# An edge layer's pair terms, laid out by quarters of the neighbours and 32 channels

## The chip, the cores and the metric

The kernel runs on one core of a Trainium2 chip. Its engines are TensorE (PE, with weight loads shown apart as PEld), VectorE (DVE), ScalarE (ACT), GpSimd (POOL) and SyncE (SP). The metric is the device time of one execution in microseconds. A measurement is the median of several runs, and one further execution was recorded by the hardware profiler; the views of the profile below are of that one.

## The reference, cut to what matters

The program is a chain of four layers on an image tensor of 4 samples, 56 rows (l), 56 columns (n) and 128 channels, in float32: an attention layer, an edge layer, a spectral layer and a convolution, each on a group-normalised input and added to it. The change touches the edge layer alone:

```python
W1, W2 = (We[:, :f], We[:, f:])                      # f = 128
proj_i = jnp.einsum('blnf,of->blno', x, W1)
proj_j = jnp.einsum('blnf,of->blno', x, W2)
edge = jax.nn.relu(proj_i[:, :, :, None, :] + proj_j[:, :, None, :, :] + be)
edge_sum = edge.sum(axis=3)
node_in = jnp.concatenate([x, edge_sum], axis=-1)
node = jax.nn.relu(jnp.einsum('blnc,oc->blno', node_in, Wn) + bn)
```

For every row l and every column n, the layer sums relu(a[n] + c[m] + be) over all 56 columns m of the same row, for each of the 128 channels. These are 4 x 56 x 56 x 56 x 128 pair terms. The sum, with x, goes through one more projection.

## The kernel before, in words

The samples are worked one after the other. For each, `fast_layer` computes the attention layer into the tile x1 and `edge_layer` works on x1 in place. Channels are the 128 partitions. The 3136 pixels of a sample are cut into 7 blocks (NBLK) of 448 (NB), 8 rows of 56, so the edge layer works 28 blocks in all.

For a block, `project` (L1184, L1186) makes two products of 448 columns in PSUM: e_pc with W2 and e_pa with W1. `evacuate` (L1194 to L1197) has ScalarE write e_c = -(e_pc) - be and e_a, a copy of e_pa, to SBUF, and prepare x for its later update. Then come 14 turns, listed in the string EDGE_TURNS. A turn makes the terms of 4 columns m at once, 128 x 1792 numbers. In the 9 "d" turns VectorE takes max(e_pa, e_c) (L1231), with e_pa read from PSUM and e_c from SBUF. As relu(a - c) = max(a, c) - c, the sum of the c of these turns is taken off later: e_rest is that sum (L1248). In the 5 "p" turns GpSimd subtracts e_c from e_a, both in SBUF (L1233), and ScalarE rectifies the result in place (L1235). All of GpSimd's operands here are in SBUF; e_a is the copy that it reads.

TensorE sums the terms by products with 32 x 32 blocks of the identity (L1238). A turn has 16 of them: one for each of its 4 columns m and each group r of 32 channels. They accumulate over all turns in the four PSUM banks of e_acc, which has a single buffer: the partitions of e_acc are the place q of m within its turn times 32 channels, its banks are the groups r. Each product is two instructions in the trace, as every float32 product here.

At the end of a block ScalarE copies e_acc to e_sums (L1250, 128 x 1792). `output` then makes e_po for the block before (L1202 to L1206): one product of x, one with e_rest and the negated weights, and four of e_sums, whose weights sum over the four places q. `project` of the block after next follows, and VectorE's `finish` (L1211) puts max(e_po, -bn) on x two blocks late, in turn 3.

The order on TensorE, ScalarE and VectorE is the order of the code (`manual_schedule`); GpSimd's is chosen when the program is built. The terms of VectorE have 7 buffers, those of GpSimd 4. e_pa and the tiles of tag "mm" (e_pc, e_po) have 2 PSUM banks each, which with e_acc makes all 8.

Of the kernel before, what the change touches and what calls it, by code (L numbers as in the profile page):

```python
# [12 lines left out]
F32 = mybir.dt.float32  # L13
AF = mybir.ActivationFunctionType
ALU = mybir.AluOpType
AX = mybir.AxisListType
# [3 lines left out]
P = 128  # L20
B = 4
HH = 56
TOK = HH * HH
NB = 448
# [8 lines left out]
def bc(ap, axis, n):  # L33

    ap = ap.unsqueeze(axis)
    shape = list(ap.shape)
    shape[axis] = n
    return ap.to_broadcast(shape)


def blk(j):
    return slice(j * NB, (j + 1) * NB)
# [149 lines left out]
def apply_norm(k, out, xt, mr):  # L192
    k.nc.vector.tensor_scalar(out, xt, mr[:, 0:1], mr[:, 1:2], ALU.subtract, ALU.mult)
# [950 lines left out]

EDGE_TURNS = "ddpddpdpddpddp"


def edge_layer(k, w, x1, st):  # L1150

    nc, tc = k.nc, k.tc
    xf = x1.rearrange("p l n -> p (l n)")
    nd = 4 * EDGE_TURNS.count("d")
    quarters = [slice(32 * q, 32 * q + 32) for q in range(4)]
    with ExitStack() as es:  # L1160
        big = es.enter_context(tc.tile_pool(name="e_big", bufs=1))
        wk = es.enter_context(tc.tile_pool(name="e_wk", bufs=2))
        psum = es.enter_context(tc.tile_pool(name="e_ps", bufs=2, space=PSUM))

        def bank():
            return psum.tile([P, 512], F32, tag="mm", name="e_mm")

        mr = group_norm_factors(k, wk, bank, st)
        xg = big.tile([P, TOK], F32, name="e_xg")
        shift = wk.tile([P, 1], F32, name="e_shift", bufs=1)  # L1170
        nc.vector.tensor_scalar(shift, mr[:, 0:1], mr[:, 1:2], -1.0, ALU.mult, ALU.mult)
        ready = {}

        def normed(j):
            if j < 2:
                apply_norm(k, xg[:, blk(j)], xf[:, blk(j)], mr)
            elif j < NBLK:
                nc.scalar.activation(xg[:, blk(j)], xf[:, blk(j)], AF.Identity, bias=shift, scale=mr[:, 1:2])

        def project(j):  # L1180
            if j >= NBLK:
                return
            pc = psum.tile([P, 512], F32, tag="mm", name="e_pc")
            nc.tensor.matmul(pc[:, :NB], w.W2, xg[:, blk(j)], start=True, stop=True)  # L1184
            pa = psum.tile([P, 512], F32, tag="pa", name="e_pa")
            nc.tensor.matmul(pa[:, :NB], w.W1, xg[:, blk(j)], start=True, stop=True)  # L1186
            ready[j] = pa, pc

        def evacuate(j):
            if j >= NBLK:  # L1190
                return
            pa, pc = ready[j]
            c = wk.tile([P, 8, HH], F32, name="e_c")
            nc.scalar.activation(c.rearrange("p l m -> p (l m)"), pc[:, :NB], AF.Identity, bias=w.nbe, scale=-1.0)  # L1194
            a = wk.tile([P, NB], F32, name="e_a")
            nc.scalar.copy(a, pa[:, :NB])  # L1196
            nc.scalar.activation(xf[:, blk(j)], xf[:, blk(j)], AF.Identity, bias=w.bn)  # L1197
            ready[j] = pa, a, c

        def output(j, rest, sums):  # L1200
            po = psum.tile([P, 512], F32, tag="mm", name="e_po")
            nc.tensor.matmul(po[:, :NB], w.Wn[:, 0, :], xg[:, blk(j)], start=True, stop=False)  # L1202
            nc.tensor.matmul(po[:, :NB].rearrange("p (l n) -> p l n", l=8), w.nWn, bc(rest, 2, HH),
                             start=False, stop=False)
            for r in range(4):
                nc.tensor.matmul(po[:, :NB], w.Wnq[:, r, :], sums[:, r, :], start=False, stop=(r == 3))  # L1206
            return po

        def finish(j, po):

            nc.vector.scalar_tensor_tensor(xf[:, blk(j)], po[:, :NB], w.nbn, xf[:, blk(j)], ALU.max, ALU.add)  # L1211

        with tc.manual_schedule(engines={mybir.EngineType.PE, mybir.EngineType.Activation, mybir.EngineType.DVE}):
            for j in range(2):
                normed(j)
            for j in range(2):
                project(j)
                evacuate(j)
            last = po = None
            for j in range(NBLK):  # L1220
                pa, a, c = ready.pop(j)
                acc = psum.tile([P, 4, 512], F32, name="e_acc", bufs=1)
                rest = wk.tile([P, 8], F32, name="e_rest")
                at = {"d": 0, "p": nd}
                for g, e in enumerate(EDGE_TURNS):
                    t = wk.tile([P, 4, 8, HH], F32, tag="e_" + e, name="e_t" + e, bufs=7 if e == "d" else 4)
                    cm = bc(c[:, :, at[e]:at[e] + 4].rearrange("p l m -> p m l"), 3, HH)
                    at[e] += 4
                    if e == "d":
                        am = bc(pa[:, :NB].rearrange("p (l n) -> p l n", l=8), 1, 4)  # L1230
                        nc.vector.tensor_tensor(t, am, cm, ALU.max)  # L1231
                    else:
                        nc.gpsimd.tensor_sub(t, bc(a.rearrange("p (l n) -> p l n", l=8), 1, 4), cm)  # L1233
                        tf = t.rearrange("p m l n -> p (m l n)")
                        nc.scalar.activation(tf, tf, AF.Relu)  # L1235
                    for q in range(4):
                        for r, o in enumerate(quarters):
                            nc.tensor.matmul(acc[quarters[q], r, :NB], k.ident[o, o],  # L1238
                                             t[o, q].rearrange("p l n -> p (l n)"),
                                             start=(g == 0), stop=(g == len(EDGE_TURNS) - 1))  # L1240
                    if g == 3 and po is not None:
                        finish(j - 2, po)
                    if g == 5 and j:
                        evacuate(j + 1)
                    if g == 8:
                        normed(j + 2)
                    if g == 9:
                        nc.vector.tensor_reduce(rest, c[:, :, 0:nd], AX.X, ALU.add)  # L1248
                sums = wk.tile([P, 4, NB], F32, name="e_sums")
                nc.scalar.copy(sums, acc[:, :, :NB])  # L1250
                if last:
                    po = output(*last)
                project(j + 2)
                last = j, rest, sums
            finish(NBLK - 2, po)
            finish(NBLK - 1, output(*last))


def edge_weights(k, w, pool):

    for n, t in (("nbe", w.be), ("nbn", w.bn), ("nWn", w.Wn[:, 1, :])):
        r = pool.tile(list(t.shape), F32, name="e_" + n)
        k.nc.vector.tensor_scalar_mul(r, t, -1.0)
        setattr(w, n, r)


def l1_host(i):
    We, Wn = i["L1_conv_We"], i["L1_conv_Wn"]
    W2 = Wn[:, P:].T.reshape(4, 1, 32, P)
    return {  # L1270
        "w1_W1": We[:, :P].T, "w1_W2": We[:, P:].T, "w1_be": i["L1_conv_be"].reshape(P, 1),
        "w1_Wn": Wn.T.reshape(2, P, P).transpose(1, 0, 2), "w1_bn": i["L1_conv_bn"].reshape(P, 1),
        "w1_Wnq": np.broadcast_to(W2, (4, 4, 32, P)).reshape(4, P, P).transpose(1, 0, 2),
    }


# [1388 lines left out]
def group_norm_factors(k, pool, bank, st):  # L2665

    nc = k.nc
    mv = pool.tile([P, 2], F32, tag="mv", name="gf_mv")
    nc.vector.bn_aggr(mv, st.rearrange("p a b -> p (a b)"))
    ps = bank()  # L2670
    nc.tensor.matmul(ps[:, 0:1], k.g4, mv[:, 0:1], start=True, stop=True)
    mr = pool.tile([P, 2], F32, tag="mr", name="gf_mr")
    nc.vector.tensor_copy(mr[:, 0:1], ps[:, 0:1])
    t = pool.tile([P, 1], F32, tag="gt", name="gf_t")
    nc.vector.tensor_sub(t, mv[:, 0:1], mr[:, 0:1])
    nc.vector.tensor_mul(t, t, t)
    nc.vector.tensor_add(t, t, mv[:, 1:2])
    ps = bank()
    nc.tensor.matmul(ps[:, 0:1], k.g4, t, start=True, stop=True)
    nc.scalar.activation(t, ps[:, 0:1], AF.Sqrt, bias=k.eps)  # L2680
    nc.vector.reciprocal(mr[:, 1:2], t)
    return mr
# [158 lines left out]
```

## Time and profile before

| | us |
|---|---|
| median of 3 runs | 3586.84 |
| lowest and highest run | 3580.55, 3589.28 |
| profiled execution, own time | 3579.81 |
| its span | 3578.0 |
| TensorE busy in the span | 3372.0 |
| VectorE busy | 2702.3 |
| ScalarE busy | 2089.9 |
| GpSimd busy | 1249.2 |
| e_td, VectorE, 252 instructions | 491.2 |
| e_tp, GpSimd, 140 instructions | 451.5 |

A group line of the profile reads: source line, engine, operation, output and inputs by the program's names, shapes, number of instructions, then busy time in us and the mean of one in ns, then the idle time of the engine just ahead of them and what ended it. A line of a timeline reads: start in us from the span's beginning, length in us, and the instructions merged in it. "Releaser" is what ended an engine's wait. Shares of busy time are means over stages with different limits, so the prediction reads the edge layer's own stretches.

### The profile page before, as it was taken

How to read it: one execution, taken by the hardware profiler on the slowest of the kernel's cores; microseconds unless marked ns; L12 is line 12 of the kernel's file. 1: busy time of each engine (PE TensorE's matmuls, PEld its weight loads, DVE VectorE, ACT ScalarE, POOL GpSimd, SP SyncE). 2: the span in 40 equal slices, each digit the busy share in tenths (PEclk: the TensorE clock that was granted, in tenths of full speed). 3: DMA queues.
4: the chain of work that ended last, by engine and by line, in shares of the span. 5: the costliest groups of instructions: out<-in, count | busy, mean ns of one | idle time of the engine just before them, and what ended most of it. 6: DMA issues, size and time to landing. Idle time of an engine off the chain costs nothing.

```text
span 3578.0 us, 80873 instructions
## 1 busy us (share of the span) xinstructions
PE 3372.0 (94%) x36096; PEld 1549.4 (43%) x36096; DVE 2702.3 (76%) x2531; ACT 2089.9 (58%) x2103; POOL 1249.2 (35%) x752
## 2 busy tenths in 40 slices
PE   6999998989999898999999999999898899999998
PEld 4433344553333455333344643333456443336664
DVE  6588868767888696688859758887784678886776
ACT  4688865458888564688856458887552112214442
POOL 1000017600000581000018400000673778884686
PEclk8999999999999999999999999999998999999999
DMA  2144420014333000444310024442103027763101
GB/s 103 43 92 92 95 42 20 20 47 94 88 88 83 20 3 20 99 93 94 89 44 3 20 57 94 94 94 63 38 3 101 15 53 178 181 148 91 55 19 55
DMA packets 98076, 244.51 MB, mean 68 GB/s; under 512 B 64456, under 2 KB 69832, under 8 KB 92712
## 3 DMA queue, kind: packets, MB, share of 16 engines
q0 software_dynamic: 16128, 102.77, 14.2%
q1 hardware_dynamic: 74872, 123.64, 11.9%
q10 hardware_dynamic: 6720, 12.85, 1.3%
q8 instruction: 285, 4.67, 0.5%
q14 instruction: 71, 0.58, 0.1%
HBM read 79.46 MB, written 31.33 MB: 31 GB/s over the span
## 4 chain that ended last, share of the span: by engine, by line
PE 79%; DVE 10%; ACT 4%; issue 4%; POOL 3%; DMA 0%; POOLq 0%; DVEq 0%; ACTq 0%
PE f_pm L818 17%; PE f_pm L684 15%; PE u_po L1878 8%; PE e_acc L1238 7%; PE q_acc L1732 3%; DVE e_td L1231 3%; PE f_pm L791 2%; PE e_po L1206 2%; PE f_pm L770 2%; ACT f_ring L821 1%; PE f_pm L464 1%; PE o_d L2141 1%; DVE f_acc L673 1%; PE o_d L2538 1%; PE f_pm L715 1%
## 5 line engine op out<-in xcount | busy, mean ns | idle before, releaser
L821 ACT ACTIVATE f_ring<-f_pm 128x1792 f32<-128x1792 f32 (+1 forms) x764 | 1093.8, 1482 | 228.7 <-PE f_pm L818 181.2
L673 DVE TENSOR_TENSOR f_acc<-f_acc,f_ring 128x1792 f32<-128x1792 f32 x468 | 947.7, 2025 | 191.1 <-ACT f_ring L821 160.9
L818 PE MATMUL f_pm<-f_qT,f_kT 32*128 32x448 f32 x5376 | 725.2, 571 | 15.5 <-ACT f_ring L821 5.1
L684 PE MATMUL f_pm<-f_ring,f_va 128*32 128x448 f32 (+1 forms) x6304 | 589.4, 490 | 0.0
L663 POOL DMA_DIRECT2D f_far<-f_ring x112 | 96.6, 862 | 1329.3 <-ACT f_ring L821 1108.2
L1231 DVE TENSOR_TENSOR e_td<-e_pa,e_c 128x1792 f32<-128x1792 f32 x252 | 491.2, 2018 | 14.1 <-ACT e_a L1196 14.1
L1233 POOL TENSOR_TENSOR e_tp<-e_a,e_c 128x1792 f32<-128x1792 f32 x140 | 451.5, 3261 | 101.4 <-PE e_acc L1238 59.8
L818 PEld LDWEIGHTS f_pm<-f_qT,f_kT 32*128 32x128 f32 x5376 | 260.4, 183 | 417.2 <-ACT f_ring L821 304.7
L1238 PE MATMUL e_acc<-e_td,t_shared 32*32 32x448 f32 x8064 | 325.8, 545 | 24.9 <-DVE e_td L1231 24.0
L684 PEld LDWEIGHTS f_pm<-f_ring,f_va 128*32 128x32 f32 x6304 | 164.2, 109 | 409.7 <-issue 397.4
L1873 DVE TENSOR_TENSOR u_ud<-u_px,u_d 112x1792 f32<-112x1792 f32 x144 | 263.5, 1864 | 39.6 <-PE u_po L1878 35.4
L1235 ACT ACTIVATE e_tp<-e_tp 128x1792 f32<-128x1792 f32 x140 | 233.4, 1694 | 74.0 <-POOL e_tp L1233 74.0
L1875 POOL TENSOR_TENSOR u_up<-xh,u_d 112x1792 f32<-112x1792 f32 (+1 forms) x72 | 240.9, 3376 | 55.0 <-PE u_po L1878 39.7
L1238 PE MATMUL e_acc<-e_tp,t_shared 32*32 32x448 f32 x4480 | 222.6, 544 | 3.0 <-ACT e_tp L1235 2.4
L1878 PE MATMUL u_po<-u_ud,AT 112*64 112x448 f32 x1056 | 213.8, 544 | 1.9 <-DVE u_ud L1873 1.9
L1238 PEld LDWEIGHTS e_acc<-e_td,t_shared 32*32 32x32 f32 x8064 | 142.3, 103 | 138.4 <-DVE e_td L1231 79.4
L1878 PEld LDWEIGHTS u_po<-u_ud,AT 112*64 112x64 f32 x1056 | 74.4, 138 | 128.8 <-issue 112.9
L1250 ACT COPY e_sums<-e_acc 128x1792 f32<-128x1792 f32 x28 | 46.3, 1652 | 136.2 <-PE e_acc L1238 136.2
L1238 PEld LDWEIGHTS e_acc<-e_tp,t_shared 32*32 32x32 f32 x4480 | 96.5, 103 | 53.0 <-issue 16.6
L728 DVE RECIPROCAL f_den<-f_den 128x448 f32<-128x448 f32 x28 | 82.6, 2951 | 44.1 <-ACT f_den L725 44.1
L1717 POOL TENSOR_TENSOR q_u<-iS,q_g 128x1792 f32<-128x1792 f32 x32 | 102.8, 3236 | 23.0 <-PE q_acc L1732 22.8
L1732 PE MATMUL q_acc<-q_u,S 64*64 64x448 f32 x1024 | 104.6, 553 | 4.4 <-DVE q_u L1719 3.3
(525 smaller groups left out, 4511.6 us busy)
## 6 DMA issues: line engine op xcount, KB each, us to landing
f_far<-f_ring POOLq DMA_DIRECT2D x112, 896.0 KB, 6.3
u_d<-dd SPq DMA_DIRECT2D x46, 784.0 KB
f_far<-f_ring SPq DMA_DIRECT2D x28, 896.0 KB
xw<-in_x SPq DMA_DIRECT2D x4, 1568.0 KB
x2d<-x SPq DMA_DIRECT2D x4, 1568.0 KB
xat<-x SPq DMA_DIRECT2D x4, 1568.0 KB
x_xs<-xat ACTq DMA_DIRECT2D x32, 196.0 KB
xm<-x_ev ACTq DMA_DIRECT2D x64, 98.0 KB
```

The lines of the kernel that those rows point to most:

```text
L673: nc.vector.tensor_add(e.acc, e.acc, slots(j, c))
L684: nc.tensor.matmul(e.po[heads[h], part], va[o, c, heads[h]], p, start=(c == 0), stop=(c == 23 and part.stop == NB))
L818: nc.tensor.matmul(ss[:, i, :NB], kT[heads[h], c * P:(c + 1) * P], qT[heads[h], blk(j)], start=True, stop=True)
L821: nc.scalar.activation(ring[:, slot:slot + m, :], ss[:, :m, :NB], AF.Exp, scale=scale)
L1231: nc.vector.tensor_tensor(t, am, cm, ALU.max)
L1233: nc.gpsimd.tensor_sub(t, bc(a.rearrange("p (l n) -> p l n", l=8), 1, 4), cm)
L1235: nc.scalar.activation(tf, tf, AF.Relu)
L1238: nc.tensor.matmul(acc[quarters[q], r, :NB], k.ident[o, o], t[o, q].rearrange("p l n -> p (l n)"), start=(g == 0), stop=(g == len(EDGE_TUR ...
L1732: nc.tensor.matmul(acc[bp][i][halves[hb % 2], hb // 2, :NB], x[o], u[o, 8 * hb:8 * hb + 8, :].rearrange("p h t -> p (h t)"), start=first, ...
L1873: nc.vector.tensor_mul(u, bc(px[:, :, :NB], 2, m), dm)
L1875: nc.gpsimd.tensor_mul(u, bc(x, 2, m), dm)
L1878: nc.tensor.matmul(po[64 * b2:64 * b2 + 64, :NB], st.AT[:, 8 * i + h0 + q, 2 * bp + b2, :], u[:, b2, q, :], start=(left == 16), stop=(left ...
```

## The change

The terms are laid out in another way. The 56 columns m are cut into 4 quarters of M = 14. The partitions of a term are now (quarter q of m, 32 channels) and its free axes are (channel group r, row l, column n). A turn g takes the columns m = g, 14 + g, 28 + g and 42 + g together.

- `project` makes e_pc in 16 products of 112 columns (32 channels by 14 columns m of 8 rows each), and e_pa in four products of 448, each with weights that hold 32 channels of W1 four times over. e_pa takes four banks, with one buffer.
- `evacuate` has ScalarE write e_c = -(e_pc) and the four groups of e_a = e_pa + be to SBUF. Of these, the second two come later, in turn 8.
- VectorE's and GpSimd's terms both read e_a and e_c, which are in SBUF.
- Of the 14 turns, 8 are VectorE's, 5 GpSimd's, and one, "s", is shared: VectorE makes its groups r = 0 and 1, GpSimd its groups 2 and 3, 128 x 896 numbers each.
- TensorE sums a term with four products of 128 rows by 32 columns: S is the 32 x 32 identity four times over, so a product sums the four quarters and leaves the group's 32 channels. e_acc is one bank with two buffers. The c terms of VectorE's turns (e_rest, now two reductions) are taken off in e_acc by four products with -S.
- e_sums is 128 x 448, and `output` has two products instead of six.
- In the first block of a layer, VectorE's first two turns are made group by group, so that they can begin with the first group of e_a.
- `edge_weights` no longer negates be and the second half of Wn; the buffers of VectorE's terms are 6 and 2 (half terms), those of GpSimd's 4 and 2.

The diff, cut to its core:

```diff
-EDGE_TURNS = "ddpddpdpddpddp"
+EDGE_TURNS = "ddpddpsdpdpddp"
...
         def project(j):
...
             pc = psum.tile([P, 512], F32, tag="mm", name="e_pc")
-            nc.tensor.matmul(pc[:, :NB], w.W2, xg[:, blk(j)], start=True, stop=True)
-            pa = psum.tile([P, 512], F32, tag="pa", name="e_pa")
-            nc.tensor.matmul(pa[:, :NB], w.W1, xg[:, blk(j)], start=True, stop=True)
-            ready[j] = pa, pc
-
-        def evacuate(j):
+            xm = xg[:, blk(j)].rearrange("p (l m) -> p l m", l=8)
+            for r, o in enumerate(quarters):
+                for q in range(4):
+                    nc.tensor.matmul(pc[quarters[q], 8 * M * r:8 * M * (r + 1)].rearrange("p (l m) -> p l m", l=8),
+                                     w.W2[:, o], xm[:, :, M * q:M * (q + 1)], start=True, stop=True)
+            pa = psum.tile([P, 4, 512], F32, name="e_pa", bufs=1)
+            for r in range(4):
+                nc.tensor.matmul(pa[:, r, :NB], w.W1[:, r, :], xg[:, blk(j)], start=True, stop=True)
+            c = wk.tile([P, 4, 8, M], F32, name="e_c")
+            a = wk.tile([P, 4, NB], F32, name="e_a")
+            ready[j] = pc, pa, c, a
+
+        def evacuate(j, part):
...
-            c = wk.tile([P, 8, HH], F32, name="e_c")
-            nc.scalar.activation(c.rearrange("p l m -> p (l m)"), pc[:, :NB], AF.Identity, bias=w.nbe, scale=-1.0)
-            a = wk.tile([P, NB], F32, name="e_a")
-            nc.scalar.copy(a, pa[:, :NB])
-            nc.scalar.activation(xf[:, blk(j)], xf[:, blk(j)], AF.Identity, bias=w.bn)
-            ready[j] = pa, a, c
+            pc, pa, c, a = ready[j]
+            if part == 0:
+                nc.scalar.activation(c.rearrange("p r l m -> p (r l m)"), pc[:, :NB], AF.Identity, scale=-1.0)
+            for r in range(2 * part, 2 * part + 2):
+                nc.scalar.activation(a[:, r, :], pa[:, r, :NB], AF.Identity, bias=w.be[:, r:r + 1])
+            if part == 1:
+                nc.scalar.activation(xf[:, blk(j)], xf[:, blk(j)], AF.Identity, bias=w.bn)
+
+        def terms(j, m, t, r0, r1, e):
...
+            _, _, c, a = ready[j]
+            cm = bc(c[:, r0:r1, :, m], 3, HH)
+            am = a[:, r0:r1, :].rearrange("p r (l n) -> p r l n", l=8)
+            if e == "d":
+                nc.vector.tensor_tensor(t, am, cm, ALU.max)
+            else:
+                nc.gpsimd.tensor_sub(t, am, cm)
+                tf = t.rearrange("p r l n -> p (r l n)")
+                nc.scalar.activation(tf, tf, AF.Relu)
...
             nc.tensor.matmul(po[:, :NB], w.Wn[:, 0, :], xg[:, blk(j)], start=True, stop=False)
-            nc.tensor.matmul(po[:, :NB].rearrange("p (l n) -> p l n", l=8), w.nWn, bc(rest, 2, HH),
-                             start=False, stop=False)
-            for r in range(4):
-                nc.tensor.matmul(po[:, :NB], w.Wnq[:, r, :], sums[:, r, :], start=False, stop=(r == 3))
+            nc.tensor.matmul(po[:, :NB], w.Wn[:, 1, :], sums, start=False, stop=True)
...
             for j in range(NBLK):
-                pa, a, c = ready.pop(j)
-                acc = psum.tile([P, 4, 512], F32, name="e_acc", bufs=1)
-                rest = wk.tile([P, 8], F32, name="e_rest")
+                acc = psum.tile([P, 512], F32, name="e_acc")
+                rest = wk.tile([P, 4, 8], F32, name="e_rest")
...
-                    cm = bc(c[:, :, at[e]:at[e] + 4].rearrange("p l m -> p m l"), 3, HH)
-                    at[e] += 4
-                    if e == "d":
-                        am = bc(pa[:, :NB].rearrange("p (l n) -> p l n", l=8), 1, 4)
-                        nc.vector.tensor_tensor(t, am, cm, ALU.max)
+                    if g in early:
+                        parts = [(early[g], 0)]
+                    elif e == "s":
+                        parts = [(tile_of("d", 2), 0), (tile_of("p", 2), 2)]
+                        for t, r in parts:
+                            terms(j, m, t, r, r + 2, "p" if r else "d")
                     else:
-                        nc.gpsimd.tensor_sub(t, bc(a.rearrange("p (l n) -> p l n", l=8), 1, 4), cm)
-                        tf = t.rearrange("p m l n -> p (m l n)")
-                        nc.scalar.activation(tf, tf, AF.Relu)
-                    for q in range(4):
-                        for r, o in enumerate(quarters):
-                            nc.tensor.matmul(acc[quarters[q], r, :NB], k.ident[o, o],
-                                             t[o, q].rearrange("p l n -> p (l n)"),
-                                             start=(g == 0), stop=(g == len(EDGE_TURNS) - 1))
+                        parts = [(tile_of(e), 0)]
+                        terms(j, m, parts[0][0], 0, 4, e)
+                    for t, r0 in parts:
+                        for r in range(t.shape[1]):
+                            nc.tensor.matmul(acc[quarters[r0 + r], :NB], w.S[:, 0, :], t[:, r].rearrange("p l n -> p (l n)"),
+                                             start=(g == 0), stop=False)
...
-                sums = wk.tile([P, 4, NB], F32, name="e_sums")
-                nc.scalar.copy(sums, acc[:, :, :NB])
+                for r in range(4):
+                    nc.tensor.matmul(acc[quarters[r], :NB].rearrange("p (l n) -> p l n", l=8), w.S[:, 1, :],
+                                     bc(rest[:, r, :], 2, HH), start=False, stop=True)
+                sums = wk.tile([P, NB], F32, name="e_sums")
+                nc.scalar.copy(sums, acc[:, :NB])
```

More of the change, by code (lines that the diff above doesn't have):

```diff
@@ L1157, in edge_layer @@
     xf = x1.rearrange("p l n -> p (l n)")
-    nd = 4 * EDGE_TURNS.count("d")
+    M = HH // 4
+    nd, ns = EDGE_TURNS.count("d"), EDGE_TURNS.count("s")
     quarters = [slice(32 * q, 32 * q + 32) for q in range(4)]
@@ L1190, in evacuate @@
+            pa = psum.tile([P, 4, 512], F32, name="e_pa", bufs=1)
[5 more added lines that the diff above has]
+        def evacuate(j, part):
             if j >= NBLK:
                 return
-            pa, pc = ready[j]
-            c = wk.tile([P, 8, HH], F32, name="e_c")
@@ L1194, in evacuate @@
-            nc.scalar.activation(c.rearrange("p l m -> p (l m)"), pc[:, :NB], AF.Identity, bias=w.nbe, scale=-1.0)
-            a = wk.tile([P, NB], F32, name="e_a")
-            nc.scalar.copy(a, pa[:, :NB])
-            nc.scalar.activation(xf[:, blk(j)], xf[:, blk(j)], AF.Identity, bias=w.bn)
-            ready[j] = pa, a, c
-        def output(j, rest, sums):
+            pc, pa, c, a = ready[j]
+            if part == 0:
+                nc.scalar.activation(c.rearrange("p r l m -> p (r l m)"), pc[:, :NB], AF.Identity, scale=-1.0)
@@ L1201, in output, with tile_of @@
+        def tile_of(e, n=4):
+            return wk.tile([P, n, 8, HH], F32, tag="e_%s%d" % (e, n), name="e_t" + e,
+                           bufs=2 if n < 4 else 6 if e == "d" else 4)
+        def output(j, sums):
             po = psum.tile([P, 512], F32, tag="mm", name="e_po")
             nc.tensor.matmul(po[:, :NB], w.Wn[:, 0, :], xg[:, blk(j)], start=True, stop=False)
-            nc.tensor.matmul(po[:, :NB].rearrange("p (l n) -> p l n", l=8), w.nWn, bc(rest, 2, HH),
-                             start=False, stop=False)
@@ L1215, in edge_layer @@
                 normed(j)
-            for j in range(2):
-                project(j)
-                evacuate(j)
+            project(0)
+            for part in range(2):
+                evacuate(0, part)
+            project(1)
             last = po = None
             for j in range(NBLK):
-                pa, a, c = ready.pop(j)
-                acc = psum.tile([P, 4, 512], F32, name="e_acc", bufs=1)
-                rest = wk.tile([P, 8], F32, name="e_rest")
-                at = {"d": 0, "p": nd}
-                for g, e in enumerate(EDGE_TURNS):
-                    t = wk.tile([P, 4, 8, HH], F32, tag="e_" + e, name="e_t" + e, bufs=7 if e == "d" else 4)
-                    cm = bc(c[:, :, at[e]:at[e] + 4].rearrange("p l m -> p m l"), 3, HH)
-                    at[e] += 4
-                    if e == "d":
-                        am = bc(pa[:, :NB].rearrange("p (l n) -> p l n", l=8), 1, 4)
-                        nc.vector.tensor_tensor(t, am, cm, ALU.max)
-                    else:
-                        nc.gpsimd.tensor_sub(t, bc(a.rearrange("p (l n) -> p l n", l=8), 1, 4), cm)
-                        tf = t.rearrange("p m l n -> p (m l n)")
-                        nc.scalar.activation(tf, tf, AF.Relu)
-                    for q in range(4):
-                        for r, o in enumerate(quarters):
-                            nc.tensor.matmul(acc[quarters[q], r, :NB], k.ident[o, o],
-                                             t[o, q].rearrange("p l n -> p (l n)"),
-                                             start=(g == 0), stop=(g == len(EDGE_TURNS) - 1))
@@ new lines, in edge_layer @@
+                acc = psum.tile([P, 512], F32, name="e_acc")
+                rest = wk.tile([P, 4, 8], F32, name="e_rest")
+                at = {"d": 0, "p": nd + ns, "s": nd}
+                early = {g: tile_of("d") for g in range(2)} if j == 0 else {}
+                for r in range(4 if early else 0):
+                    for g, t in early.items():
+                        terms(j, at["d"] + g, t[:, r:r + 1], r, r + 1, "d")
+                for g, e in enumerate(EDGE_TURNS):
+                    m = at[e]
+                    at[e] += 1
+                    if g in early:
[4 more added lines that the diff above has]
+                            terms(j, m, t, r, r + 2, "p" if r else "d")
+                    else:
+                        parts = [(tile_of(e), 0)]
[4 more added lines that the diff above has]
+                                             start=(g == 0), stop=False)
@@ L1241, in edge_layer @@
                     if g == 3 and po is not None:
                         finish(j - 2, po)
-                    if g == 5 and j:
-                        evacuate(j + 1)
+                    if g == 5:
+                        evacuate(j + 1, 0)
                     if g == 8:
+                        evacuate(j + 1, 1)
+                    if g == 10:
                         normed(j + 2)
-                    if g == 9:
-                        nc.vector.tensor_reduce(rest, c[:, :, 0:nd], AX.X, ALU.add)
@@ L1249, in edge_layer @@
-                sums = wk.tile([P, 4, NB], F32, name="e_sums")
-                nc.scalar.copy(sums, acc[:, :, :NB])
+                    if g == 8:
+                        if ns:
+                            nc.vector.tensor_reduce(rest[:, 0:2], ready[j][2][:, 0:2, :, 0:nd + 1], AX.X, ALU.add)
+                        nc.vector.tensor_reduce(rest[:, 2 if ns else 0:4], ready[j][2][:, 2 if ns else 0:4, :, 0:nd], AX.X, ALU.add)
+                for r in range(4):
+                    nc.tensor.matmul(acc[quarters[r], :NB].rearrange("p (l n) -> p l n", l=8), w.S[:, 1, :],
+                                     bc(rest[:, r, :], 2, HH), start=False, stop=True)
@@ L1253, in edge_layer @@
                 project(j + 2)
-                last = j, rest, sums
+                last = j, sums
             finish(NBLK - 2, po)
@@ L1259, in edge_weights @@
 def edge_weights(k, w, pool):
[L1261 to L1264, printed above, removed]
+    w.nbn = pool.tile([P, 1], F32, name="e_nbn")
+    k.nc.vector.tensor_scalar_mul(w.nbn, w.bn, -1.0)
 def l1_host(i):
     We, Wn = i["L1_conv_We"], i["L1_conv_Wn"]
-    W2 = Wn[:, P:].T.reshape(4, 1, 32, P)
+    W1 = np.broadcast_to(We[:, :P].T.reshape(P, 4, 1, 32), (P, 4, 4, 32)).reshape(P, 4, P)
+    S = np.tile(np.eye(32, dtype=np.float32), (4, 1))
     return {
-        "w1_W1": We[:, :P].T, "w1_W2": We[:, P:].T, "w1_be": i["L1_conv_be"].reshape(P, 1),
+        "w1_W1": W1, "w1_W2": We[:, P:].T, "w1_be": np.tile(i["L1_conv_be"].reshape(4, 32).T, (4, 1)),
         "w1_Wn": Wn.T.reshape(2, P, P).transpose(1, 0, 2), "w1_bn": i["L1_conv_bn"].reshape(P, 1),
-        "w1_Wnq": np.broadcast_to(W2, (4, 4, 32, P)).reshape(4, P, P).transpose(1, 0, 2),
+        "w1_S": np.stack((S, -S), 1),
     }
```

## The prediction

> **What bounds the kernel now.** I read the page first: the chain that ended last and the costliest groups.
>
> ```profile
> PE 79%; DVE 10%; ACT 4%; issue 4%; POOL 3%; DMA 0%; POOLq 0%; DVEq 0%; ACTq 0%
> ...
> L1231 DVE TENSOR_TENSOR e_td<-e_pa,e_c 128x1792 f32<-128x1792 f32 x252 | 491.2, 2018 | 14.1 <-ACT e_a L1196 14.1
> L1233 POOL TENSOR_TENSOR e_tp<-e_a,e_c 128x1792 f32<-128x1792 f32 x140 | 451.5, 3261 | 101.4 <-PE e_acc L1238 59.8
> ...
> L1250 ACT COPY e_sums<-e_acc 128x1792 f32<-128x1792 f32 x28 | 46.3, 1652 | 136.2 <-PE e_acc L1238 136.2
> ```
>
> TensorE carries four fifths of the chain. The edge layer runs four times (once per sample) over seven blocks, 28 blocks in all. So I asked for the busy time of each engine in two blocks of the first one (columns: stretch, its length, then PE, PEld, DVE, ACT, POOL).
>
> ```profile
> 599.74:619.42 19.68, 19.68 (x481) 11.72 (x474) 18.42 (x12) 12.08 (x11) 16.14 (x5) 1.00 0.01 3
> 619.42:639.10 19.68, 19.68 (x481) 11.71 (x474) 18.42 (x12) 12.09 (x11) 16.14 (x5) 1.00 0.01 3
> ```
>
> A block takes 19.68 us and TensorE is busy in all of it: 14 turns of about 0.96 (13.5), twelve e_po instructions start to start 0.376 (4.5), four for e_pc and e_pa (1.5). VectorE has 18.42, GpSimd 16.14, almost all of it side by side. That overlap is what matters here. VectorE's max reads e_pa, which is in PSUM, and e_c in SBUF; GpSimd's subtraction reads e_a and e_c, both in SBUF. Beside it GpSimd stretches nothing: the 252 instructions of e_td lie between 2.014 and 2.027 us.
>
> **What the trace says of two SBUF inputs.** The change makes VectorE read e_a instead of e_pa, so I looked for places where VectorE reads two SBUF tensors while GpSimd does too. They are few and agree. Timelines of VectorE, then GpSimd (start us, us):
>
> ```profile
> 2857.87 1.09 DVE L1758 TENSOR_TENSOR y<-y,q_red 128x896 f32<-128x896 f32 x1
> ...
> 2860.28 2.68 DVE L1766 TENSOR_TENSOR y<-y,q_den 128x896 f32<-128x896 f32 x1
> ```
>
> ```profile
> 2857.92 4.09 POOL L1717 TENSOR_TENSOR q_u<-iS,q_g 128x1792 f32<-128x1792 f32 x1
> 2869.70 3.19 POOL L1717 TENSOR_TENSOR q_u<-iS,q_g 128x1792 f32<-128x1792 f32 x1 [7.69 <-PE q_acc L1732]
> ```
>
> L1717 began 0.05 us behind L1758 and took 4.09 instead of 3.19: it lost the 0.9 us that a product of 1.09 needs. Then L1766, started while L1717 ran, took 2.68 instead of 1.09: it ended 0.95 us after L1717 did, and 896 elements need about that. So the two run one after the other, whichever began first, and nothing is gained from the overlap but the waiting one's fixed 0.14 us. The end of each sample's MLP shows it again:
>
> ```profile
> 542.06 1.02 DVE L799 SCALAR_TENSOR_TENSOR xf<-xf,t_first,xw 128x392 f32<-128x392 f32 x1
> ```
>
> ```profile
> 541.75 0.91 POOL L804 TENSOR_TENSOR x<-xf,xw 128x343 f32<-128x343 f32 x1 [3.95 <-DVE xf L793]
> 542.62 0.58 POOL L805 TENSOR_TENSOR x<-xf,xw 128x28 f32<-128x28 f32 x1
> ```
>
> L799 (0.63 for its like, L793, with a PSUM input) waits for L804 to end at 542.66; L805 (0.24 in its other executions) then waits for L799 to end at 543.08. All four samples show the same. And where GpSimd has work queued back to back, VectorE gets no turn between: this subtraction of one element per partition needs 0.16 us and sat through nine GpSimd instructions.
>
> ```profile
> 2723.54 5.46 DVE L1458 TENSOR_TENSOR s_t<-s_mv,s_mr 128x1 f32<-128x1 f32 x1
> ```
>
> The Trainium skill (page "SBUF — State Buffer", section "Who interferes with whom") speaks against this change in the same sense: VectorE's second SBUF read and GpSimd share a port, and whoever has it keeps it for the whole instruction. It goes further than these few rows, as it says so of every such pair; by the rule a block costs the sum of both engines' times, worked out below from rows as 34.2 us, and without it the longer one, 17.9.
>
> **The change part by part**, for one block.
>
> *VectorE and GpSimd.* Nine and five turns become 8.5 and 5.5. Back to back, VectorE's spacing is 1.93 us (five took 9.74, the last 2.02 of it), GpSimd's 3.22 (five in 16.14, the last 3.26). For half a turn the nearest rows are VectorE's 128x896 (1.09, about 1.00 back to back) and GpSimd's 128x896, L1758 (1.69, about 1.65). Held port time: VectorE 8 x 1.93 + 1.00 = 16.4; GpSimd 5 x 3.22 + 1.65 = 17.75. Sum **34.2**. Lower end: with strict alternation each hides its fixed part (1.88 and 0.95, 3.05 and 1.50): 32.7. Upper end: VectorE's one-input work, finish 0.68 and two small reduces at up to 0.3, is not covered by a GpSimd term: 35.5. I take 34.2, the back-to-back rows, since GpSimd was seen to keep its turn while it has work; the one-input instructions then lie beside GpSimd.
>
> *TensorE.* A turn becomes four products of 128 rows by 32 columns (eight instructions for 32). That form is in the trace: L684 starts a group of four heads, eight instructions, 0.70 us after the one before. 14 turns and the four products with e_rest: 15 x 0.70 = 10.5. e_po: four instructions instead of twelve, 1.5. e_pa: eight instead of two, 3.0. e_pc: sixteen pieces of 112 columns on four column groups, about 0.7. Sum 15.7, 4 us less than now, but hidden: the pair of engines needs 34.2.
>
> *ScalarE.* 5.5 rectifications (9.3), e_c 0.63, four e_a at 0.53, x 0.67, e_xg 0.75, e_sums of 448 elements about 0.53: 14. Hidden as well.
>
> *Waits and buffers.* e_acc is now doubled, so TensorE no longer waits for e_sums; that costs and brings nothing under 34.2. Behind a VectorE term that waits for GpSimd stand finish and the reduces, for which nobody hurries. With six and four buffers, one of the two engines has work whenever the other is short of a buffer, so I count the port as never idle.
>
> *Ends of a layer.* Start: TensorE runs four e_pa products at a low clock (granted 0.61 between 549.2 and 553.6) and VectorE starts in pieces of 448: +0.8. End: before, VectorE's last term ended at 687.5 and the layer at 699.7, 12.2 us, with e_sums 1.65 and two e_po groups of 4.5. After: last turn and e_rest 1.9, the older e_po 1.5, the last 1.5, finish 0.68: 5.7 with e_sums beside it.
>
> *Sum.* The first layer began its terms at 553.7. After: 553.7 + 0.8 + 7 x 34.2 + 5.7 = 799.6 against 699.7, +99.9; four layers **+400**. The profiled execution took 3579.81 us, its span 3578.0; the median of the runs is 3586.84, 7 more. A change of 400 gives 3980 there and **3987** against the median.
>
> The edits at the start of the kernel (one VectorE negation of 128x128 less, a pack of other size) are below a microsecond and I count them as nothing; no DMA is moved.
>
> **Rivals.**
>
> *The exclusion doesn't hold for this pair* (it is shown here by a handful of instructions, none of them a stream). Then a block is bound by the longer of VectorE (16.4 + 0.68 + 0.6 = 17.7) and GpSimd (17.75), with handovers 17.9. A layer: 553.7 + 0.8 + 7 x 17.9 + 5.7 = 685.5, 14.2 less; four give -57: **3530**. It decides as soon as e_td stays at 2.02 beside e_tp. For it: TensorE, which is the bound now, is relieved by 4 us a block. Against it: every pair in the trace with two SBUF inputs on both sides. This is the case on the other side.
>
> *The exclusion holds and the port also idles.* If GpSimd's runs leave TensorE and ScalarE to catch up while both producers lack buffers, one rectification and one turn, 1.7 + 0.75, are added once or twice a block: 28 x 2.45 to 4.9 = 69 to 137 more, **4056 to 4124**. For it: L1458, one engine kept out for long. Against it: ten buffered turns.
>
> *TensorE's clock drops because it idles.* At the 0.61 of the layer's start, 15.7 becomes 25.7, still under 34.2; only the ends of a layer grow, by about 3 us each, 12 in all. That is inside the range.
>
> That the change would not do what it says is out: e_td's first operand is the SBUF tile e_a in the diff.
>
> **How the numbers follow.** Forecast 0.80: 32.7 to 35.5 a block, with 3 us more at each layer's end for the upper one, give 3944 to 4035. Idle port 0.12, no exclusion 0.06, something between that cancels 0.02. The range goes a little below the first and takes in half of the second: 3925 to 4085. A difference of 0.3% is about what a measurement of this kernel can tell from none: faster 0.06, same 0.02, slower 0.92.
>
> **What the profile after would show.** Right: e_td and e_tp both longer in the mean than 2.02 and 3.26, with the excess of one lying under the other; blocks of about 34 us with TensorE busy in about half; the attention layers and all behind the edge layer unchanged. Wrong: e_td at 2.02 with blocks near 18 (first rival), or blocks over 36 with gaps on both VectorE and GpSimd (second). The TensorE step is wrong if a turn takes much more than 0.7 us of starts; it would not show in the time.

## The result, and the profile after

| | before | after |
|---|---|---|
| median of 4 runs, us | 3585.96 | 3981.27 |
| lowest and highest | 3580.55, 3589.28 | 3977.35, 3995.76 |
| profiled execution, its span | 3579.81, 3578.0 | 3984.77, 3983.0 |
| the four edge layers together | 603.5 | 1002.4 |
| all the rest of the span | 2974.5 | 2980.6 |

The changed kernel takes 1.1116 times as long, with a 95% interval of 1.1093 to 1.1139. The forecast was 3987. The last two rows are read off the timelines: an edge layer runs from the start of e_shift (VectorE, L1171 before, L1173 after) to the end of its last update of x (L1211 before, L1234 after). The edge layers take 398.9 us more; the rest differs by 6, and in the runs below, which change the edge layer alone, it lies between 2965 and 2987, so those 6 are no finding.

The page of the kernel after: the chain that ended last by engine, then the groups that answer to those shown of before.

```profile
PE 63%; DVE 23%; issue 7%; ACT 4%; POOL 2%; DMA 0%; DVEq 0%; POOLq 0%; ACTq 0%
...
L1216 DVE TENSOR_TENSOR e_td<-e_a,e_c 128x1792 f32<-128x1792 f32 (+2 forms) x276 | 924.6, 3412 | 28.1 <-ACT e_a L1206 28.1
L1218 POOL TENSOR_TENSOR e_tp<-e_a,e_c 128x1792 f32<-128x1792 f32 (+1 forms) x168 | 716.2, 4287 | 239.3 <-PE e_acc L1266 176.7
...
L1284 ACT COPY e_sums<-e_acc 128x448 f32<-128x448 f32 x28 | 14.9, 532 | 525.1 <-PE e_acc L1281 525.1
```

VectorE's share of the chain went from 10% to 23%. The mean of e_td rose from 2018 to 3412 ns although it now contains half and quarter terms, the mean of e_tp from 3261 to 4287 ns. Busy time here contains waiting inside the instruction, so a longer instruction is not more work. GpSimd was idle for 239 us ahead of its terms, 177 of them until TensorE had used up an older one and its buffer was free (the rest was the wait for e_a at the four starts), so it was not the only limit; VectorE was hardly ever idle, with 28 us ahead of its terms in four layers.

The busy time of each engine in the first edge layer and in two stretches of about a block (stretch, length, then PE, PEld, DVE, ACT, POOL, granted clock):

```profile
556.70:799.40 242.70, 151.58 (x1086) 44.89 (x1076) 237.62 (x91) 90.47 (x94) 179.26 (x46) 0.81 0.00 1
585.00:619.00 34.00, 21.57 (x168) 6.66 (x160) 34.00 (x10) 13.27 (x14) 31.78 (x8) 0.75 0.00 0
650.00:687.00 37.00, 23.34 (x176) 6.84 (x168) 37.00 (x10) 17.97 (x19) 35.11 (x9) 0.83 0.00 1
```

VectorE is busy all the time in both stretches of blocks, TensorE in under two thirds, where it was busy throughout a block before. The terms of the seven blocks run from 556.70 to 792.96, 33.75 us a block against 19.68. The last column but two, the granted clock, is below full speed. It doesn't make the loss: TensorE is free for a third of these stretches and VectorE doesn't wait for it. More on the clock at the end.

How the two engines take turns is seen in a timeline of some 20 us, VectorE first, then GpSimd. The second line of each is one instruction alone. The first of VectorE's five is shorter (3.54 us): beside it GpSimd made only a half term.

```profile
654.17 23.52 DVE L1216 TENSOR_TENSOR e_td<-e_a,e_c 128x1792 f32<-128x1792 f32 x5
...
657.63 5.07 DVE L1216 TENSOR_TENSOR e_td<-e_a,e_c 128x1792 f32<-128x1792 f32 x1
```

```profile
655.79 20.03 POOL L1218 TENSOR_TENSOR e_tp<-e_a,e_c 128x1792 f32<-128x1792 f32 x4
...
660.78 5.03 POOL L1218 TENSOR_TENSOR e_tp<-e_a,e_c 128x1792 f32<-128x1792 f32 x1
```

From there on GpSimd starts one every 5.0 us and VectorE too: the term at 657.63 ends at 662.70, that of GpSimd at 660.78 began 1.9 us before this and ends 3.1 us after it. Each instruction is 5.05 us long, of which it works 1.9 (VectorE) or 3.1 (GpSimd) and waits the rest.

### The profile page after: what moved, and what is told of

It is laid out like the page before. It is cut to its first block, busy times and chain, and to the rows that moved or that the text cites. A ratio compares the mean times of both kernels' runs of the same rounds, so it can differ in the third digit from the quotient of the medians.

```text
span 3983.0 us, 64261 instructions
## 1 busy us (share of the span) xinstructions
PE 3443.8 (86%) x27696; PEld 1439.5 (36%) x27696; DVE 3140.5 (79%) x2581; ACT 2123.2 (53%) x2215; POOL 1514.5 (38%) x780
## 4 chain that ended last, share of the span: by engine, by line
PE 63%; DVE 23%; issue 7%; ACT 4%; POOL 2%; DMA 0%; DVEq 0%; POOLq 0%; ACTq 0%
DVE e_td L1216 16%; PE f_pm L818 16%; PE f_pm L684 14%; PE u_po L1911 7%; PE q_acc L1765 3%; PE f_pm L791 2%; PE f_pm L770 2%; ACT f_ring L821 1%; PE e_acc L1266 1%; PE e_pa L1194 1%; PE f_pm L464 1%; PE o_d L2174 1%; DVE f_acc L673 1%; PE o_d L2571 1%; PE f_pm L715 1%
## 5 line engine op out<-in xcount | busy, mean ns | idle before, releaser
L1216 DVE TENSOR_TENSOR e_td<-e_a,e_c 128x1792 f32<-128x1792 f32 (+2 forms) x276 | 924.6, 3412 | 28.1 <-ACT e_a L1206 28.1
L1218 POOL TENSOR_TENSOR e_tp<-e_a,e_c 128x1792 f32<-128x1792 f32 (+1 forms) x168 | 716.2, 4287 | 239.3 <-PE e_acc L1266 176.7
L1266 PE MATMUL e_acc<-e_td,t_edge 128*32 128x448 f32 x1904 | 297.5, 667 | 351.5 <-DVE e_td L1216 350.9
L1284 ACT COPY e_sums<-e_acc 128x448 f32<-128x448 f32 x28 | 14.9, 532 | 525.1 <-PE e_acc L1281 525.1
L1220 ACT ACTIVATE e_tp<-e_tp 128x1792 f32<-128x1792 f32 x168 | 257.9, 1572 | 41.2 <-POOL e_tp L1218 40.7
L1266 PEld LDWEIGHTS e_acc<-e_td,t_edge 128*32 128x32 f32 x1904 | 53.2, 119 | 563.7 <-DVE e_td L1216 508.9
L1266 PE MATMUL e_acc<-e_tp,t_edge 128*32 128x448 f32 x1232 | 205.9, 693 | 0.0
L804 POOL TENSOR_TENSOR x<-xf,xw 128x343 f32<-128x343 f32 x28 | 25.5, 912 | 226.4 <-DVE xf L793 226.4
```

The lines of the kernel that those rows point to most:

```text
L1218: nc.gpsimd.tensor_sub(t, am, cm)
L1266: nc.tensor.matmul(acc[quarters[r0 + r], :NB], w.S[:, 0, :], t[:, r].rearrange("p l n -> p (l n)"), start=(g == 0), stop=False)
```

## The experiments

The theory: VectorE's second SBUF operand excludes GpSimd's SBUF reads, and this alone makes the loss. Below, "port time" is the time for which a term of one engine keeps the other waiting. Rivals: the new layout with its products on TensorE, the shared turn, or the slower TensorE clock makes it. All kernels that follow ran beside runs of the kernel before; ratios are to those. Where a table gives a layer, "start" is from e_shift to the first term, "terms" to the end of the last term, "tail" to the last update of x.

**The kernel before, with e_a from SBUF.** One operand is changed; layout, turns and products are those of before.

```diff
-                        am = bc(pa[:, :NB].rearrange("p (l n) -> p l n", l=8), 1, 4)
+                        am = bc(a.rearrange("p (l n) -> p l n", l=8), 1, 4)
```

> The kernel before with one operand changed: VectorE's max reads e_a (SBUF) instead of e_pa (PSUM); nothing of the new layout. Theory (two SBUF inputs on VectorE and on GpSimd exclude each other): in the changed kernel a pair of one VectorE and one GpSimd term is 5.0 us from start to start; five pairs and four more VectorE terms at 1.93 are 32.7, with finish and the reduce about 33.3 a block instead of 19.7, 28 x 13.6 = 380 more: about 3967 us. Rival (the new layout, its strides or the products of 128 rows by 32 columns slow the engines): nothing of it is in here, so about 3586 us, with e_td at 2.02.

Measured: 3976.19 us, ratio 1.1089 (1.1071 to 1.1108). All instructions of the two terms (count, then shortest, median and longest in ns):

```profile
L1231 DVE TENSOR_TENSOR e_td<-e_a,e_c x252: 2006/5016/5084, 553.6 to 3072.7; 128x1792 f32<-128x1792 f32 x126
L1233 POOL TENSOR_TENSOR e_tp<-e_a,e_c x140: 3250/5026/5135, 553.7 to 3059.5; 128x1792 f32<-128x1792 f32 x140
```

This one operand gives nearly the whole loss, in a kernel without the new layout and without a shared turn. In before the 252 instructions all lay between 2014 and 2027 ns; now their median is 5016.

**The changed kernel, with one operand of VectorE in PSUM.** e_pc is made with negated weights, so that it is e_c itself; VectorE reads it in PSUM and e_a in SBUF. ScalarE still copies it for GpSimd. e_pc keeps two PSUM banks for this, and e_po and e_acc have one each.

```diff
+            if e == "d":
+                c = pc[:, :NB].rearrange("p (r l m) -> p r l m", r=4, l=8)
...
-                nc.scalar.activation(c.rearrange("p r l m -> p (r l m)"), pc[:, :NB], AF.Identity, scale=-1.0)
+                nc.scalar.copy(c.rearrange("p r l m -> p (r l m)"), pc[:, :NB])
...
-                                     w.W2[:, o], xm[:, :, M * q:M * (q + 1)], start=True, stop=True)
+                                     w.nW2[:, o], xm[:, :, M * q:M * (q + 1)], start=True, stop=True)
```

> The changed kernel with one operand moved: e_pc is made with -W2 and VectorE reads its c terms from e_pc in PSUM, so that it has one SBUF input; GpSimd reads the copy e_c. e_pc keeps its two banks, e_po and e_acc have one buffer each. Theory (exclusion): e_td back to 2.02 and e_tp to 3.26, a block at 17.9 (VectorE 17.7, GpSimd 17.75), about 3530 us; 3515 to 3560 with the single e_acc. Rival (layout, or TensorE's lower clock): e_td and e_tp stay long, blocks near 34, about 3980 us.

Measured: 3559.70 us, ratio 0.9922 (0.9905 to 0.9939). The two terms, GpSimd's timeline in the first layer, and one block, from finish to finish (L1236):

```profile
L1218 DVE TENSOR_TENSOR e_td<-e_a,e_pc x276: 610/2012/2022, 560.4 to 2648.7; 128x1792 f32<-128x1792 f32 x108, 128x448 f32<-128x448 f32 x16, 128x896 f32<-128x896 f32 x14
L1220 POOL TENSOR_TENSOR e_tp<-e_a,e_c x168: 1713/3277/3332, 562.1 to 2648.2; 128x1792 f32<-128x1792 f32 x140, 128x896 f32<-128x896 f32 x28
```

```profile
562.07 124.54 POOL L1220 TENSOR_TENSOR e_tp<-e_a,e_c 128x1792 f32<-128x1792 f32 x42 [14.41 <-ACT e_a L1206]
```

```profile
620.68:638.47 17.79, 17.64 (x168) 6.44 (x171) 17.53 (x12) 13.37 (x15) 17.79 (x7) 1.00 0.00 1
```

Neither engine waits for the other inside a term any more: e_td is 2012 ns beside a GpSimd that works through all 42 of its terms without a gap. The block is 17.79 us. So all that the change does besides the operand is worth a little under 1%, in the good direction and with fewer PSUM buffers, and the operand costs 421.6 us. The run also rules out that the engines clash because they read the same tile: here both still read e_a from SBUF, and in before both read e_c. The Trainium skill (page "SBUF — State Buffer", section "Who interferes with whom") says that a VectorE instruction with at most one SBUF input doesn't contend with GpSimd, unless it runs in one of the modes that take both of VectorE's ports; these 276 instructions agree.

**The changed kernel, all turns VectorE's.** GpSimd makes no term.

```diff
-EDGE_TURNS = "ddpddpsdpdpddp"
+EDGE_TURNS = "dddddddddddddd"
```

> The changed kernel with all fourteen turns on VectorE, none on GpSimd or shared. Theory (exclusion): nobody to wait for, 14 x 1.93 + 1.3 = 28.3 a block instead of 33.75, 28 x 5.4 = 152 less: about 3830 us, so that GpSimd's 5.5 turns cost more than they carry. Rival (VectorE's terms are slow by themselves in this layout): 14 at the mean 3.4 of the changed kernel, 48 a block, about 4380 us.

Measured: 3820.92 us, ratio 1.0653 (1.0635 to 1.0671). The first layer (columns as above):

```profile
560.00:756.50 196.50, 141.56 (x1071) 35.85 (x1060) 196.30 (x116) 28.49 (x52) 0.00 (x0) 0.89 0.00 1
```

Without GpSimd's terms the kernel is some 160 us faster than with them. A block takes 196.8/7 = 28.1 us, 14 terms of 1.93 and the small instructions. As the two engines work one after the other, a term by GpSimd costs 3.05 to 3.1 us and one by VectorE 1.9. GpSimd's help is then worth less than nothing. The fourth layer shows the exclusion on other tiles: its terms took 209.0 us instead of 196.8. In its first 52 us GpSimd made tiles for the spectral layer (operations of at most 128x512, none of which reads e_a or e_c), and twelve of VectorE's terms took 2.4 to 3.0 us instead of 2.0.

**The changed kernel without a shared turn**, with the nine and five turns of before.

```diff
-EDGE_TURNS = "ddpddpsdpdpddp"
+EDGE_TURNS = "ddpddpdpddpddp"
```

> The changed kernel with the turns of before, nine for VectorE and five for GpSimd, none shared. Theory (exclusion): half a turn costs 1.0 us of the port on VectorE and 1.5 to 1.65 on GpSimd, so a block is 0.5 to 0.65 shorter than with the shared turn, 14 to 18 us less: about 3965 us. Rival (the engines lie beside each other and VectorE is the bound): half a turn more on VectorE, 28 x 1.0 more, about 4009 us.

Measured: 3963.20 us, ratio 1.1054 (1.1035 to 1.1072). Terms of a layer: 231.6 us instead of 236. The intervals of this run and of the changed kernel don't overlap, so moving half a turn to GpSimd costs about 18 us: half a term is 1.5 us of GpSimd's port time instead of 0.95 of VectorE's, 0.55 a block or 15 in all (an estimate from the rows of the prediction).

**Both together: c in PSUM, nine and five turns.** The two diffs above in one kernel; without exclusion the shared turn should balance the two engines, and taking it away cost.

> The kernel that takes VectorE's c terms from PSUM, with nine turns for VectorE, five for GpSimd, none shared. It prices the shared turn where the two engines lie beside each other. Theory (without the exclusion the longer engine bounds a block): VectorE 9 x 1.93 + 0.57 + 0.6 = 18.55 instead of GpSimd's 17.79, 28 x 0.76 = 21 more than 3560: about 3580 us, a little less as GpSimd ends earlier in a layer's last block. Rival (something else bounds a block, TensorE or the single e_acc): no difference, 3560 us.

Measured: 3544.18 us, ratio 0.9906 (0.989 to 0.9923). This is a miss: the block got longer as expected, the kernel didn't. VectorE's and GpSimd's timelines:

```profile
619.00 0.69 DVE L1236 SCALAR_TENSOR_TENSOR x<-e_po,e_nbn,x 128x448 f32<-128x448 f32 x1
...
637.33 0.70 DVE L1236 SCALAR_TENSOR_TENSOR x<-e_po,e_nbn,x 128x448 f32<-128x448 f32 x1
```

```profile
560.69 61.33 POOL L1220 TENSOR_TENSOR e_tp<-e_a,e_c 128x1792 f32<-128x1792 f32 x19 [15.27 <-ACT e_a L1206]
624.20 16.15 POOL L1220 TENSOR_TENSOR e_tp<-e_a,e_c 128x1792 f32<-128x1792 f32 x5 [2.18 <-PE e_acc L1268]
```

From finish to finish 18.33 us, against 17.79 with the shared turn, and GpSimd has gaps (2.18 us ahead of 624.20) while VectorE has none. But a layer is 142.8 us long in both kernels: terms 127.6 and tail 7.49 here, terms 126.2 and tail 8.46 there. With the shared turn GpSimd is the bound, and it starts 1.7 us after VectorE at each layer and its last term has still to be rectified. What sharing saves in the middle is lost at the ends. The medians of the two, 3544 and 3560, differ by the rest of the span: in the traces the four edge layers take 571.4 and 571.2 us, all the rest 2970.0 and 2986.8.

**c in PSUM, and e_pa in four tiles of a bank.** In the changed kernel ScalarE's first copy e_a waited for all four products of e_pa, though it reads the first bank alone. The start of the changed kernel's first layer in the timelines of TensorE, ScalarE and VectorE:

```profile
550.84 5.16 PE L1194 MATMUL e_pa<-e_xg,t_edge 128*128 128x448 f32 x8
```

```profile
556.03 2.21 ACT L1206 ACTIVATE e_a<-e_pa,t_edge 128x448 f32<-128x448 f32 x4 [4.51 <-PE e_pa L1194]
```

```profile
556.70 27.99 DVE L1216 TENSOR_TENSOR e_td<-e_a,e_c 128x448 f32<-128x448 f32 x12 [7.14 <-ACT e_a L1206]
```

The edit, on top of the kernel with c in PSUM:

```diff
-            pa = psum.tile([P, 4, 512], F32, name="e_pa", bufs=1)
+            pa = [psum.tile([P, 512], F32, tag="pa%d" % r, name="e_pa", bufs=1) for r in range(4)]
```

> The kernel that takes VectorE's c terms from PSUM, with the four groups of e_pa as four tiles of one bank each. In the changed kernel the first copy of e_a began at 556.03, when the last product of e_pa had ended, not the first, so that VectorE started at 556.7 where 553.7 was forecast. Theory (the copies wait for the whole tile, and GpSimd, which needs all four groups, starts the bound): VectorE starts about 3 us earlier, GpSimd about 1.6; the bound is GpSimd, so four layers give 6.5 less than 3560: about 3553 us. Rival (VectorE's start is what counts): 12 less, 3548. Rival (the copies wait for TensorE's order, not the tile): no difference.

Measured: 3546.69 us, ratio 0.991 (0.9893 to 0.9927). ScalarE in the first layer:

```profile
552.70 2.89 ACT L1206 ACTIVATE e_a<-e_pa,t_edge 128x448 f32<-128x448 f32 x4 [1.17 <-PE e_pa L1194]
```

The products start at nearly the same time, and the first copy comes at 552.70 instead of 556.03; the first term is 4.9 us after e_shift instead of 7 to 8.6. So the wait was for the tile, not for the bank. In the layer this is 2 us, 8 in all, which the trace shows and the ratios are too wide to show.

**Short ends as well.** On top of that, the last e_po of a layer takes a free bank of e_pc, so that it needn't wait for the e_po before it, and the products with e_rest are issued in turn 11 instead of after the last turn.

```diff
-            po = psum.tile([P, 512], F32, tag="mm", name="e_po", bufs=1)
+            last_one = j == NBLK - 1
+            po = psum.tile([P, 512], F32, tag="pc" if last_one else "mm", name="e_po", bufs=2 if last_one else 1)
...
+                    if g == 11:
+                        for r in range(4):
+                            nc.tensor.matmul(acc[quarters[r], :NB].rearrange("p (l n) -> p l n", l=8), w.S[:, 1, :],
+                                             bc(rest[:, r, :], 2, HH), start=False, stop=False)
```

> As the kernel with the four tiles for e_pa, and at the end of a layer the last e_po in a bank of its own, so that it doesn't wait for the finish of the block before, and the products with e_rest ahead of the last turns. Theory: 1.5 and 0.75 us off each layer's end, four layers 9 less: about 3544 us. Rival (the end is bound by GpSimd's last term, its rectification and sums alone): 3553 us.

Measured: 3539.43 us, ratio 0.9889 (0.9873 to 0.9906). TensorE at the end of the first layer:

```profile
680.60 0.93 PE L1285 MATMUL e_acc<-e_rest,t_edge 128*32 128x448 f32 x8
...
682.29 0.96 PE L1269 MATMUL e_acc<-e_tp,t_edge 128*32 128x448 f32 x8
683.18 1.02 PE L1231 MATMUL e_po<-e_xg,t_edge 128*128 128x448 f32 x2
```

The products with e_rest now lie ahead of the last turn, and e_po follows that turn at once. The tail is 6.67 us instead of 8.46. This version beats both kernels, the one before by 1.1%. Its step from the kernel ahead of it is 7.3 us in the medians on the same chip, and four tails make 7.2; the two intervals overlap, so that the trace and not the ratio carries this step.

**Shorter pieces on VectorE.** In the changed kernel VectorE's term is made in four instructions of 448 elements, to see whether the length of an instruction sets how the two share.

```diff
-                nc.vector.tensor_tensor(t, am, cm, ALU.max)
+                for i in range(r1 - r0):
+                    nc.vector.tensor_tensor(t[:, i], am[:, i], cm[:, i], ALU.max)
```

> The changed kernel (both engines read SBUF) with each VectorE term made as pieces of 448 numbers, one per group, 34 a block. It asks how the two take turns. Theory (one instruction each, in strict turn, as its 5.0 us pairs look): while GpSimd has work, a piece waits for one GpSimd term, about 3.1 + 0.47 = 3.6 us, and a GpSimd term for one piece, 3.5; the port's total stays 32.7 to 35.1 a block, so 3955 to 4020 us. Rival (GpSimd keeps the port while it has work, as the 5.46 us of the one-element subtraction look): pieces of 6 us and more. Rival (the port is shared by time): several pieces beside one term, GpSimd's terms near 5.

Measured: 4027.74 us, ratio 1.1249 (1.123 to 1.1268), a little above what was expected. GpSimd, then VectorE, in one stretch:

```profile
602.80 15.93 POOL L1219 TENSOR_TENSOR e_tp<-e_a,e_c 128x1792 f32<-128x1792 f32 x1 [4.26 <-PE e_acc L1267]
```

```profile
602.16 13.46 DVE L1217 TENSOR_TENSOR e_td<-e_a,e_c 128x448 f32<-128x448 f32 x25
615.54 0.30 DVE L1279 TENSOR_REDUCE e_rest<-e_c 128x16 f32<-128x144 f32 x1
615.75 0.28 DVE L1280 TENSOR_REDUCE e_rest<-e_c 128x16 f32<-128x128 f32 x1
615.94 3.28 DVE L1217 TENSOR_TENSOR e_td<-e_a,e_c 128x448 f32<-128x448 f32 x1
```

One subtraction of GpSimd lasts 15.93 us: VectorE's pieces go on at 0.54 us each, 23 of them begun after GpSimd's instruction. It ends at 618.73, 3.2 us after the first small reduction of VectorE, which has one SBUF input. In other stretches the two take turns, a term of GpSimd and a piece of VectorE, with a pair every 3.6 us, as the median of GpSimd's terms (shortest, median, longest in ns) shows:

```profile
L1219 POOL TENSOR_TENSOR e_tp<-e_a,e_c x168: 2092/3630/15975, 562.8 to 3110.7; 128x1792 f32<-128x1792 f32 x140, 128x896 f32<-128x896 f32 x28
```

The trace says when each of the two happens. Of the 168 terms 24 took over 6 us. All 24 came after a pause of GpSimd, while it waited for a buffer, and all ended about 3.2 us after VectorE next began an instruction with one SBUF input (a reduction or a finish). Every term that followed GpSimd's last one without a pause took turns. The reverse doesn't hold: 28 other terms came after a pause too and took 3.3 to 4.4 us. The skill's section named above says that the order of issue decides who blocks; in the 24 it doesn't, since pieces that began later went first.

## Why the prediction was right, step by step

*What bounds the kernel now, and that it would change hands.* Right. VectorE and GpSimd, one after the other, take TensorE's place as the bound, and one operand decides it: put in the old layout it makes 1.1089, taken out of the new one it leaves 0.9922. The handful of pairs that the trace of before held told the price of a stream of them.

*The block, 34.2 us.* Right within 0.45 us: 33.75, the mean of the seven. The bounds of 32.7 and 35.5 hold it. The reason for the choice inside them was wrong: "since GpSimd was seen to keep its turn while it has work". With terms of 1792 elements the engines take strict turns, pairs at 5.0 us, which is the sum of the two lengths without the part that waiting hides (1.88 + 3.05 = 4.93). So 32.7 was nearly the right sum for the terms. Of the 1.0 on top of it, about 0.4 us a block (0.35 to 0.45 by layer) is work of VectorE with one input (finish and two reductions, 0.67 + 0.29 + 0.27) beside which no GpSimd term ran; most of the rest, by estimate, is handing over, as pairs take 5.0 and not 4.93, and VectorE's terms in a row 1.94 and not 1.88. That 34.2 was near is in part luck: the back-to-back rows charge each term its fixed part, which it hides, and so happened to pay for the gaps that the sum left out. L1458 in before, which waited 5.46 us, was read as a rule; the run with pieces shows the same 24 times with the engines exchanged, and terms of 1792 elements never do it (none of GpSimd's took over 5.05 us).

*The port never idle.* Nearly right. GpSimd lacked buffers for 176.7 us of the four layers, and in that time VectorE ran at 1.94 a term. Only the 0.4 us a block named above had neither engine on a term; VectorE's busy time of 34.00 in 34.00 us doesn't show it, as it counts finish and the reductions.

*TensorE, 15.7 us, and hidden.* Hidden is right, the size is wrong. In the kernel with c in PSUM, at full clock, it is busy for 17.64 of the 17.79 us: a turn takes 0.75 us of starts, not 0.70, e_pa 3.2 and e_pc 0.95. "4 us less than now" was 2. It stayed hidden under 33.75, but in the rival without exclusion TensorE would have been all but the bound.

*ScalarE, 14 us.* Between 13.3 and 18 in the stretches shown, depending on how many rectifications fall in; hidden.

*Ends of a layer.* Both too short. Start: the first term at 554.5 forecast, 556.70 measured. I had e_a follow its own product; it waited for the whole tile e_pa (552.70 against 556.03 in the runs above). Tail: 5.7 forecast, 6.44 measured, since two turns, VectorE's last and GpSimd's behind it, had still to be summed, where one was counted. In the layer's end the three errors, +2.2, -3.1 and +0.7, nearly cancel: 799.6 forecast, 799.40 measured. The total is better than its terms, which is luck.

*Sum.* Forecast +400 for four layers, +398.9 measured. In the medians it is 395.3, or 11.0%: 3981.27 where 3987 was forecast.

*The rivals.* "The exclusion doesn't hold for this pair" is refuted by the length of e_td and by the experiments. Its price of 3530 was too low as well: with the exclusion taken away the kernel takes 3560, mainly because the ends are longer than I had them (start 7.0 to 8.6 against 5.4, tail 8.46 against 5.7; the terms, 126.2, are within 1 us of the forecast). The single buffer of e_po in that kernel is part of the tail: its last two finishes are 2.55 us apart, in the changed kernel 1.50. "The port also idles" by 2.45 to 4.9 us a block is refuted: blocks are 33.75, not over 36, and VectorE has no gap in them. "TensorE's clock drops" happened, at 0.81 rather than 0.61, and cost nothing in the blocks, where VectorE had no wait, nor in the tail of the first layer, where a turn's eight products took 0.94 us as at full clock.

*What the change is worth without its operand.* After less before is +395 us: +422 for the operand, -26 for all the rest of the edit. Within that rest, the shared turn costs 18 while the exclusion lasts and nothing that could be measured without it.

## What to carry to other kernels

Before a tensor operand of VectorE is moved from PSUM to SBUF, look whether GpSimd reads SBUF at the same time: here this one operand turned 17.8 us a block of parallel work into 33.75 in sequence, and giving all the work to VectorE was then faster than sharing it. The lengths of the instructions in the trace tell it at once: when those of both engines have the same median, near the sum of what each takes alone, they take turns. A copy out of a PSUM tile of several banks can wait for the last product into that tile; where the first bank is wanted early, give it a tile of its own.

## What the runs showed of the hardware that was not expected

**Who gets the port next.** Streams of 128 x 1792 on both sides alternate one for one. A stream of 128 x 448 on VectorE alternates too as long as GpSimd works without a pause; a GpSimd term that comes after a pause can be kept out for up to 16.0 us, in all 24 cases until VectorE's next instruction with one SBUF input. Why 28 other terms after a pause got in early is not settled; no run here tells it apart.

**TensorE's clock.** In the edge layer TensorE works in bursts, and the granted clock is 0.81 in the first layer from its first term to its end, 0.75 and 0.83 in the stretches shown; with all turns VectorE's it is 0.89, with c in PSUM 1.00. TensorE was busy in 62% (first layer after), 72% (all turns VectorE's) and 99% (c in PSUM) of the stretches shown. The busy share alone doesn't set the clock: the stretches with 0.75 and 0.83 both have 63%, and the first layer's terms in the run with short pieces have 73% and only 0.81. What does is not shown; no run varied it alone. The products with e_rest (L1281) take 952 ns in the median, where the kernel with c in PSUM has 539. Here TensorE had over a third of the time free, so that this is hidden; a kernel in which it has just enough would probably feel it; no run here shows one.
